# Last group's v with whole products P2 and P3, two copies moved to ScalarE, and no opening products of zeros: a two-layer graph network

## The chip, the cores and the metric

The kernel runs on one core of a Trainium2 chip, in one launch, in float32 throughout. The metric is the device time of one execution in microseconds (us). TensorE (PE) multiplies, VectorE (DVE), ScalarE (ACT) and GpSimd (POOL) work on tiles, and SyncE (SP) issues the DMAs. Each engine takes its own instructions strictly in the written order and waits where one of them needs the result of another engine.

## The reference

The inputs are `x` (128 graphs, 128 nodes, 512 features) and one symmetric 128x128 matrix `adj` of zeros and ones. Two layers follow one another, each with a residual and a normalization over the features:

```python
# layer 0
q = einsum('bnd,ed->bne', x, Wq); k = ...Wk; v = ...Wv
rel = adjacency.T * einsum('bnd,bmd->bnm', q, k)
rel = rel / norm(rel, axis=2)
x = layernorm(x + einsum('bnm,bmd->bnd', rel, v))
# layer 1: 8 heads of 64
q, k, v = x @ Wq + bq, x @ Wk + bk, x @ Wv + bv
w = softmax(q k^T / 8 + mask(adj), per head)
x = layernorm(x + w v)
```

## The kernel before, in words

**Groups and rounds.** The 128 graphs are cut into 32 groups of four, so that a group has 512 tokens and every projection is a 512x512x512 product. In a round of the schedule, layer 0 of the next group and layer 1 of the present one are interleaved. Layer 0 needs two projections: `m` (x times the product of Wq and Wk, which the kernel builds once at the start as M, line 200) and `v0`. Layer 1 needs `q`, `k` and `v1`.

**A projection** is class `Projection`. It is done in Winograd's form with seven products P1 to P7 of 256x256x256 blocks in place of eight, in the order 1, 5, 6, 2, 3, 7, 4 (`step`, lines 437 to 474). One such product is four matmuls of 128x128 weights against 256 columns (`product`, line 365). It needs sums of weight blocks (`weight_sums`, lines 156 to 160) and of token blocks (`token_sums`, lines 225 to 232), and VectorE or ScalarE folds its PSUM bank into the output. Products P2 and P3 need no sums and are split once more: each becomes seven products of 128x128x128 (`inner`, line 408; matmul in line 406), whose results VectorE adds in small pieces (lines 412 and 432), six additions for P2 and six for P3. This needs sums of 128x128 weight blocks (`inner_weight_sums`, line 148), and the last of these writes over the block `w[3]` of the weights themselves (line 154). Where `self.plain` is set, P2 and P3 are whole products with one addition each (lines 455 to 466); that is so for `m` and `v0` of group 0 alone.

**Order.** Everything is issued under a manual schedule. `dense` gives each projection step a position, and `short` gives every other piece of work one (`at`, line 778); a round is 35 positions long, and the pieces are issued by rising position, so the position decides the order on every engine's queue at once. The tables `ZERO`, `STEADY`, `QUICK` (round of the group before the last) and `LAST` (last group) hold the positions. PSUM tiles come from two pools that rotate, `ps_a` with two buffers and `ps_m` with six.

**The start.** `layer0_weights` (lines 178 to 204) first fills a tile with zeros and multiplies it by itself four times on TensorE into a bank that nobody reads. Then VectorE and ScalarE reorder the four chunks of Wq as they arrive, VectorE transposes the four quarters of Wv (line 192), transposes the first quarter of the first group's x (`x_transpose(0, 0, 0)`, line 194, instruction at line 219), and computes the sums of the Wv blocks (lines 157 to 160). TensorE meanwhile builds M. The other three quarters of x follow from the schedule.

**The end.** The last group has no later work to lie beside. Its softmax weights are transposed on TensorE against the identity (line 691) rather than by way of DRAM: two transposed halves `pwT` per graph, each copied from PSUM to SBUF (line 693). Seven of these eight copies are VectorE's, and the last one is ScalarE's. Per graph `b` the work is: scores (line 669), masking (674) and maximum (677) on VectorE, exponentials on ScalarE (684), transposition, products with v (708), scaling by the sums (713), residual (715 or 717), statistics (504, 505), the small steps of the standard deviation on GpSimd (509 to 519), normalization and store. In the same stretch the four graphs of the group before are finished (lines 607 to 654).

Of the kernel before, what the change touches and what calls it, by code (L numbers as in the profile page):

```python
# [8 lines left out]
F32 = mybir.dt.float32  # L9
# [9 lines left out]
def kernel(  # L19
# [122 lines left out]
    def inner_weight(key, o, i):  # L142
        if i >= 5:
            return wd[key][:, o - 2, i - 5]
        e, d = {1: (0, 0), 2: (0, 1), 3: (1, 0), 4: (1, 1)}[i]
        return wc[key][:, o - 1, d, e * P:(e + 1) * P]

    def inner_weight_sums(key, eng):
        for o in (2, 3):
            w = [None] + [inner_weight(key, o, i) for i in range(1, 8)]  # L150
            eng.tensor_tensor(w[5], w[3], w[4], op=ALU.add)
            eng.tensor_tensor(w[6], w[5], w[1], op=ALU.subtract)
            eng.tensor_tensor(w[7], w[1], w[3], op=ALU.subtract)
            eng.tensor_tensor(w[3], w[2], w[6], op=ALU.subtract)
# [21 lines left out]
    v21 = two.tile([P, 2, HF], F32, tag="wT", name="v21")  # L176

    def layer0_weights():

        z = one.tile([P, HF], F32, tag="wl", name="zeros")  # L180
        nc.gpsimd.memset(z, 0.0)
        pz = ps_m.tile([P, HF], F32, tag="m", name="pz")
        for _ in range(4):
            nc.tensor.matmul(pz, z[:, :P], z, start=True, stop=True)
        wq_p = one.tile([P, C, C, A, Q], F32, tag="v1", name="wq0_p")
        for ec in range(C):
            copy = nc.scalar.copy if ec % 2 else nc.vector.tensor_copy
            copy(wq_p[:, ec], quadrants(wq_s[:, ec]))
        for h in range(2):
            for dh in range(2):  # L190
                dst = wc["v0"][:, 3 if h else 1] if dh else v21 if h else wc["v0"][:, 0]
                nc.vector.transpose(dst.rearrange("p c (t s) -> p c t s", s=Q),
                                    wv_s[:, h, :, :, 2 * dh:2 * dh + 2, :].rearrange("p b a c r -> p c (b a) r"))
        x_transpose(0, 0, 0)
        weight_sums(wc["v0"], v21, nc.vector)
        p = [ps_a.tile([P, D], F32, tag="a", name=f"pM_{dc}") if dc < 2 else
             ps_m.tile([P, D], F32, tag="m", name=f"pM_{dc}") for dc in range(C)]
        for ec in range(C):
            for dc in range(C):
                nc.tensor.matmul(p[dc], wq_p[:, ec, dc].rearrange("p q r -> p (q r)"), quadrants(wk_s[:, ec]),  # L200
                                 start=(ec == 0), stop=(ec == C - 1))
        for dc in range(C):
            for e in range(2):
                place(wc["m"], m21, dc, e, p[dc][:, e * HF:(e + 1) * HF], nc.scalar.copy)
# [43 lines left out]
    def x_transpose(g, dh, h):  # L248
        if dh == 0 and h == 0:

            XT[g] = one.tile([P, C, G, P], F32, tag="xT" if g else "x1T", name=f"xT_{g}")
        if dh == 0 and h == 1:
            TX[g] = one.tile([P, 4, 2, HF], F32, tag="tx" if g else "tx1", name=f"tx_{g}")
        if dh == 1 and h == 0 and g:
            UX[g] = one.tile([P, 2, 4, P], F32, tag="ux", name=f"ux_{g}")
        transpose_quarter(XT[g], g, h, dh)
        if dh == 1 and g:
            inner_token_sums(UX[g], XT[g], 2 + h)
        if h:
            token_sums(TX[g], XT[g], dh, nc.gpsimd if g > 1 else nc.vector)  # L260
# [55 lines left out]
    class Projection:  # L316
# [8 lines left out]
        def begin(self):  # L325
            k, g = self.kind, self.g
            x0 = k in ("m", "v0")
            self.xT, self.t = (XT[g], TX[g]) if x0 else (X1T[g], TX1[g])

            self.plain = x0 and g == 0  # L330

            self.late = k == "v1" and g < NG - 1
            if self.late:
                self.s0 = one.tile([P, 2, HF], F32, tag="rel", name=f"s0_{self.name}")
            else:
                self.place()
                self.s0 = self.out(0, 0)
# [348 lines left out]
    def last_transpose(g, b, s):  # L686
        if b % 2 == 0 and s == 0:
            LT[b // 2] = one.tile([P, 2, H, P], F32, tag="tx1" if b else "x1T", name=f"wT_{g}_{b}")
        p = ps_m.tile([P, H // 2, P], F32, tag="m", name=f"pwT_{g}_{b}_{s}")
        for a in range(H // 2):  # L690
            nc.tensor.transpose(p[:, a, :], SOFT[g, b][0][:, s * (H // 2) + a, :], ident)
        copy = nc.scalar.copy if b == G - 1 and s else nc.vector.tensor_copy
        copy(LT[b // 2][:, b % 2, s * (H // 2):(s + 1) * (H // 2), :], p)

    def last_out(g, b, s):
# [37 lines left out]
    def last_store(g, b):  # L733
# [20 lines left out]
        (49, (50.5, 55, 55, 55, 55), (56.5, 58), 60.5, (64.5, 67, 69, 74.5, 76, 82, 83, 85.5)),  # L754
    )
    QUICK = (
        (31.5, (32, 33.5, 34.5, 34.5, 35), (35, 38), 40.5, (41, 43.5, 43.5, 47.5, 48.5, 50.5, 50.5, 52.5)),
        (36, (37, 37, 37, 37, 37), (39.5, 40.5), 41.5, (44.5, 45.5, 47.5, 50, 52, 53, 55, 62)),
        (37, (37.5, 41, 41, 41, 41), (41, 41), 45.5, (47.5, 50, 57.5, 57.5, 57.5, 59, 59.5, 64)),
        (37, (39, 41.5, 42.5, 44, 47), (44, 47), 49.5, (51, 52, 57.5, 61, 61, 64.5, 68.5, 68.5)),  # L760
    )
    LAST = (
        (17, (17, 17.5), (22, 22), (24, 24.5), 29, 35, 37.5),
        (17.5, (18, 19.5), (24, 25), (28.5, 33.5), 40.5, 48.5, 48.5),
        (19.5, (20, 23.5), (28.5, 29), (31, 37), 41.5, 51, 51.5),
        (23, (26.5, 26.5), (30.5, 31), (33.5, 41.5), 51, 51, 52.5),
    )


# [8 lines left out]
    def at(r, k, f, *a):  # L778
        short.setdefault(R * r + k, []).append((f, a))
# [14 lines left out]
    for g in range(NG):  # L794

        for h in range(2):
            if g:
                at(g - 2, 12, load_staged, g, h)
                at(g - 1, 12 + 4 * h, load, g, h)
        last = g == NG - 1  # L800

        sc, no, ou, de, ln, sp, st, tr = ZERO[0 if g == 0 else 2 if last else 1]
        for h in range(2):
            at(g - 1, sp[h], x1_spill, g, h)
            at(g - 1, st[h], x1_stage, g, h)
        for i, (dh, h) in enumerate(halves):
            if g or i:
                at(g - 2, ((25.5, 27, 28.5, 30) if g != 1 else (22, 23, 24, 25))[i], x_transpose, g, dh, h)
            at(g - 1, tr[i], x1_transpose, g, dh, h)
        for b in range(G):  # L810
            at(g - 1, sc[b], l0_score, g, b)
            at(g - 1, ou[b], l0_out, g, b)
            at(g - 1, ln[b // 2], l0_layernorm, g, b)
        at(g - 1, no, l0_norm, g)
        at(g - 1, de, l0_rstd, g)

        if last:
            at(g, 2, last_residual, g)
        for b in range(G):
            if last:  # L820
                sc, e, t, o, st, no, w = LAST[b]
                at(g, sc, last_scores, g, b)
                for i in range(2):
                    at(g, e[i], last_exp, g, b, i)
                    at(g, t[i], last_transpose, g, b, i)
                    at(g, o[i], last_out, g, b, i)
                at(g, st, last_stats, g, b)
                at(g, no, last_norm, g, b)
                at(g, w, last_store, g, b)
                continue  # L830
            s, ex, sp, st, pk = QUICK[b] if g == NG - 2 else STEADY[b]
            at(g, s, attn_scores, g, b)
            at(g, ex[0], attn_max, g, b)
            for i in range(4):
                at(g, ex[i + 1], attn_exp, g, b, 2 * i)
            for i in range(2):
                at(g, sp[i], attn_spill, g, b, i)
            at(g, st, attn_stage, g, b)
            pieces = attn_transpose, attn_out, attn_back, attn_rows, attn_sum, attn_stats, attn_norm, attn_write
            for k, f in zip(pk, pieces):  # L840
                at(g, k, f, g, b)
                if f is attn_rows:
                    at(g, RES if g < NG - 2 and b < 2 else k, attn_res, g, b)
# [3 lines left out]
    for k, name, eng in ((9, "v0", nc.vector), (17, "m", nc.vector), (28, "q", nc.gpsimd), (49.5, "k", nc.gpsimd),  # L847
                         (52, "v1", nc.gpsimd)):
        at(-1, k, inner_weight_sums, name, eng)

    with tc.manual_schedule():
        layer0_weights()
        for k in sorted({*short, *dense}):
            if k == -R:
                weight_sums(wc["m"], m21, nc.vector)
                for name, key in (("v", "v1"), ("q", "q")):
                    layer1_weights(name, key)
            for f, a in short.get(k, ()):
                f(*a)
            if k in dense:  # L860
                pr, i = dense[k]
                pr.step(i)
# [29 lines left out]
```

## Time and profile before

| | |
|---|---|
| median of five executions | 2450.43 us (2445.81 to 2452.06) |
| the profiled execution, time | 2451.07 us |
| its span, first to last instruction | 2449.1 us |
| TensorE busy in the span | 2425.7 us (99%) |
| VectorE busy | 1975.6 us (81%) |
| ScalarE busy | 1012.6 us (41%) |
| GpSimd busy | 1139.9 us (47%) |
| mean granted TensorE clock | 0.996 |

A float32 matmul appears in the trace as two passes, each a weight load (PEld) and a MATMUL, so the four matmuls of one product are eight records ("x8"). Records on TensorE overlap, since one starts before the one ahead has drained; how fast TensorE goes is read from the distance of the starts, not from the mean duration. A line of the timeline gives the start, the duration, the engine, the line of the kernel and the operation with its operands, and in brackets how long the engine had been idle and what it waited for. The chain view follows the work that ended last back through its releasers. The stretch view gives the busy time of each engine in a stretch, then the granted clock, the share of the DMA engines and the bytes.

### The profile page before, as it was taken

To read this page: it belongs to the slowest core of one execution; us is meant where nothing else is said; L and a number is where in the kernel's file an instruction comes from. 1 tells how busy PE (TensorE), PEld (TensorE's weight loads), DVE (VectorE), ACT (ScalarE), POOL (GpSimd) and SP (SyncE) were. 2 spreads that over 40 slices of the span, in tenths; PEclk is the share of its full clock that TensorE was granted. 3 is DMA by queue.
4 is the path that set the end of the run, shared out by engine and by line. 5 is a ranking of instruction groups with operands and counts; after the bars stand their busy time and mean duration, and the time that the engine had idled before them with its cause. 6 is when DMAs were issued, how large, how long until landed. Compare 5 with 4: busy or idle time off the path is not lost.

```text
span 2449.1 us, 48459 instructions
## 1 busy us (share of the span) xinstructions
PE 2425.7 (99%) x16560; PEld 2136.1 (87%) x16560; DVE 1975.6 (81%) x4409; ACT 1012.6 (41%) x3211; POOL 1139.9 (47%) x1797
## 2 busy tenths in 40 slices
PE   8999999999999999999999999999999999999997
PEld 6889888888888898888888888888888888888886
DVE  6678888788888788887888887888878888878887
ACT  1234443443444443444434434434444344344354
POOL 3625535345444455343454344553444543435544
PEclk9999999999999999999999999999999999999999
DMA  7356665666565666556665656665656656566564
GB/s 160 93 132 168 175 176 160 177 168 164 171 180 156 171 173 176 170 164 172 173 166 169 180 156 169 173 173 168 173 164 173 166 173 179 157 171 174 153 174 128
DMA packets 508600, 405.17 MB, mean 165 GB/s; under 512 B 37568, under 2 KB 424768, under 8 KB 508352
## 3 DMA queue, kind: packets, MB, share of 16 engines
q1 hardware_dynamic: 508352, 402.08, 59.7%
q8 instruction: 129, 2.11, 0.4%
q14 instruction: 119, 0.97, 0.1%
HBM read 237.31 MB, written 164.63 MB: 164 GB/s over the span
## 4 chain that ended last, share of the span: by engine, by line
PE 96%; DVE 2%; issue 0%; DMA 0%; SPq 0%; POOL 0%; POOLq 0%; ACT 0%; DVEq 0%
PE pa_v L365 18%; PE pa_q L365 9%; PE pa_m L365 9%; PE pa_k L365 9%; PE pc_v L406 8%; PE ps L549 5%; PE po L607 5%; PE pst L484 5%; PE pb_v L365 5%; PE po L529 4%; PE pc_k L406 4%; PE pc_q L406 4%; PE pc_m L406 4%; PE pb_q L365 2%; PE pb_k L365 2%; PE pb_m L365 2%
## 5 line engine op out<-in xcount | busy, mean ns | idle before, releaser
L575 ACT ACTIVATE w<-w,nmax 128x128 f32<-128x128 f32 x992 | 384.0, 395 | 116.0 <-DVE nmax L568 115.9
L509 POOL TENSOR_SCALAR ve<-st 128x1 f32<-128x1 f32 (+1 forms) x160 | 46.0, 287 | 746.2 <-DVE st L505 735.1
L365 PE MATMUL pa_v<-wc_v,tx 128*128 128x256 f32 x1536 | 363.8, 380 | 0.0
L365 PEld LDWEIGHTS pa_v<-wc_v,tx 128*128 128x128 f32 x1536 | 277.2, 190 | 30.9 <-issue 0.6
L524 ACT ACTIVATE xr<-xr,sh,rstd 128x512 f32<-128x512 f32 x58 | 47.2, 815 | 411.4 <-POOL sh L519 411.4
L575 ACT ACTIVATION_READ_ACCUMULATOR w<-w,nmax 128x1 f32 x992 | 191.8, 193 | 0.0
L365 PE MATMUL pa_m<-tx,wc_m 128*128 128x256 f32 x768 | 186.8, 387 | 3.2 <-DVE yT L461 2.2
L412 DVE TENSOR_TENSOR v<-pc_v,v 128x256 f32<-128x256 f32 (+1 forms) x444 | 135.2, 310 | 58.3 <-PE pc_v L406 46.4
L365 PEld LDWEIGHTS pa_q<-tx,wc_q 128*128 128x128 f32 x768 | 143.2, 190 | 44.4 <-issue 29.3
L365 PE MATMUL pa_k<-tx,wc_k 128*128 128x256 f32 x768 | 181.8, 380 | 0.0
L365 PE MATMUL pa_q<-tx,wc_q 128*128 128x256 f32 x768 | 181.6, 379 | 0.2 <-DVE qT L461 0.2
L558 DVE SCALAR_TENSOR_TENSOR w<-ps,mask 128x512 f32<-128x512 f32 x248 | 153.2, 680 | 7.3 <-PE ps L549 7.3
L365 PEld LDWEIGHTS pa_m<-tx,wc_m 128*128 128x128 f32 x768 | 140.1, 192 | 20.1 <-DVE yT L461 2.6
L568 DVE TENSOR_REDUCE nmax<-w 128x4 f32<-128x512 f32 x248 | 157.2, 675 | 0.0
L594 DVE STREAM_TRANSPOSE wT<-wl 128x1024 f32<-128x1024 f32 x124 | 154.0, 1242 | 0.3 <-DMA xl_x<-in_x_dram 0.3
L365 PEld LDWEIGHTS pa_k<-tx,wc_k 128*128 128x128 f32 x768 | 138.4, 190 | 14.9
L638 POOL TENSOR_TENSOR xr<-xr,bv_b 128x512 f32<-128x512 f32 x58 | 73.8, 1272 | 144.8 <-DMA xr<-x1d 83.9
L376 ACT ACTIVATE qT<-pa_q,bq_sb 128x256 f32<-128x256 f32 x128 | 53.7, 471 | 204.9 <-PE pa_q L365 200.2
L406 PE MATMUL pc_v<-wd_v,ux 128*128 128x128 f32 x756 | 135.8, 275 | 0.2 <-DVE v L412 0.2
L412 DVE TENSOR_TENSOR qT<-pc_q,qT 128x128 f32<-128x128 f32 (+1 forms) x320 | 96.5, 309 | 44.4 <-PE pc_q L406 36.7
L529 PE MATMUL po<-v,rel 128*128 128x512 f32 x256 | 130.7, 594 | 0.0
L549 PE MATMUL ps<-kT,qT 64*128 64x128 f32 x1984 | 129.5, 279 | 0.0
(231 smaller groups left out, 6180.9 us busy)
## 6 DMA issues: line engine op xcount, KB each, us to landing
wd<-w SPq DMA_DIRECT2D x248, 256.0 KB, 3.1
wl<-wd SPq DMA_DIRECT2D x496, 128.0 KB, 3.1
xl_x<-in_x_dram SPq DMA_DIRECT2D x256, 128.0 KB, 5.9
x<-in_x_dram SPq DMA_DIRECT2D x64, 512.0 KB, 4.7
x1d<-x SPq DMA_DIRECT2D x64, 512.0 KB, 3.1
xl_h<-x1d SPq DMA_DIRECT2D x256, 128.0 KB, 2.9
od<-oT SPq DMA_DIRECT2D x496, 64.0 KB, 2.1
o<-od SPq DMA_DIRECT2D x118, 256.0 KB, 3.0
```

The source lines that it names most:

```text
L365: nc.tensor.matmul(bank[:, m, :], l[:, k, m * P:(m + 1) * P], r[:, k, :], start=start and m == 0 and k == 0, stop=(m == 1 and k == 1), ski ...
L406: nc.tensor.matmul(self.c[o][:, slot, :], l, r, start=start, stop=True, skip_group_check=True)
L412: nc.vector.tensor_tensor(y, self.c[o][:, slot], s if kept else y, op=ALU.add)
L484: nc.tensor.matmul(p, XT[g][:, dc, b, :], YT[g][:, dc, b, :], start=(dc == 0), stop=(dc == C - 1))
L529: nc.tensor.matmul(p, REL[g][0][:, b, :], V0[g][:, b, :], start=True, stop=True)
L549: nc.tensor.matmul(p[s][:, :, a, :], QT[g][r, a, b, :], KT[g][r, a, b, :], start=True, stop=True)
L558: nc.vector.scalar_tensor_tensor(w[:, s].rearrange("p q a r -> p (q a r)"), p[s].rearrange("p q a r -> p (q a r)"), HD ** -0.5, mask, op0= ...
L568: nc.vector.tensor_reduce(nmax[:, s * (H // 2):(s + 1) * (H // 2)], w[:, s].rearrange("p q a r -> p a q r"), axis=AX.XY, op=ALU.max, negat ...
L575: nc.scalar.activation(w[:, s, :, a, :], w[:, s, :, a, :], AF.Exp, bias=nmax[:, i:i + 1], accum_out=sums[:, i:i + 1])
L594: nc.vector.transpose(wT, SOFT[g, b][0].rearrange("p a i r -> p i a r"))
L607: nc.tensor.matmul(p[s * HD:(s + 1) * HD, a, :], V1[g][:, b, h * HD:(h + 1) * HD], wT[:, s * (H // 2) + a].rearrange("p q t -> p (q t)"), ...
L638: nc.gpsimd.tensor_tensor(xr, xr, bv_b, op=ALU.add)
```

## The change

Five things change. The opening zeros and their four products go. The first quarter of x of group 0 is no longer transposed ahead of the sums of the Wv blocks; it is issued from the schedule with the other three, behind them. `v1` of the last group is `plain`: P2 and P3 are whole products. As the weight block `w[3]` has been written over by then, two 128x128 blocks of it are copied aside on GpSimd when the sums are made, and copied back on GpSimd in the last round. Of the eight copies of transposed softmax weights in the last group ScalarE takes three instead of one: the second half of graph 2 and both of graph 3. Last, the positions in `QUICK` and `LAST` are set anew.

```diff
+    kept = const.tile([P, 2, P], F32, name="kept")
+    def restore(key):
+        for o in (2, 3):
+            nc.gpsimd.tensor_copy(inner_weight(key, o, 3), kept[:, o - 2])
     def inner_weight_sums(key, eng):
         for o in (2, 3):
             w = [None] + [inner_weight(key, o, i) for i in range(1, 8)]
+            if key == "v1":
+                eng.tensor_copy(kept[:, o - 2], w[3])
...
     def layer0_weights():
-        z = one.tile([P, HF], F32, tag="wl", name="zeros")
-        nc.gpsimd.memset(z, 0.0)
-        pz = ps_m.tile([P, HF], F32, tag="m", name="pz")
-        for _ in range(4):
-            nc.tensor.matmul(pz, z[:, :P], z, start=True, stop=True)
...
-        x_transpose(0, 0, 0)
         weight_sums(wc["v0"], v21, nc.vector)
...
-            self.plain = x0 and g == 0
+            self.plain = (x0 and g == 0) or (k == "v1" and g == NG - 1)
...
-        copy = nc.scalar.copy if b == G - 1 and s else nc.vector.tensor_copy
+        copy = nc.scalar.copy if b + s >= G - 1 else nc.vector.tensor_copy
...
     QUICK = (
-        (31.5, (32, 33.5, 34.5, 34.5, 35), (35, 38), 40.5, (41, 43.5, 43.5, 47.5, 48.5, 50.5, 50.5, 52.5)),
-        (36, (37, 37, 37, 37, 37), (39.5, 40.5), 41.5, (44.5, 45.5, 47.5, 50, 52, 53, 55, 62)),
-        (37, (37.5, 41, 41, 41, 41), (41, 41), 45.5, (47.5, 50, 57.5, 57.5, 57.5, 59, 59.5, 64)),
-        (37, (39, 41.5, 42.5, 44, 47), (44, 47), 49.5, (51, 52, 57.5, 61, 61, 64.5, 68.5, 68.5)),
+        (31.5, (32, 33.5, 34.5, 34.5, 34.5), (35, 37.5), 40.5, (40.5, 43.5, 43.5, 47.5, 48.5, 50.5, 51.5, 52.5)),
+        (36, (37, 37, 37, 37, 37), (39.5, 40.5), 41.5, (44.5, 45.5, 47.5, 50, 52, 53, 55, 61.5)),
+        (37, (37.5, 41, 41, 41.5, 41.5), (41, 41.5), 45.5, (47.5, 49.5, 57.5, 57.5, 57.5, 59, 59, 66)),
+        (37, (39, 41.5, 42.5, 46, 47), (44, 47), 49.5, (51, 52.5, 57.5, 61, 61, 65.5, 68.5, 68.5)),
     )
     LAST = (
-        (17, (17, 17.5), (22, 22), (24, 24.5), 29, 35, 37.5),
-        (17.5, (18, 19.5), (24, 25), (28.5, 33.5), 40.5, 48.5, 48.5),
-        (19.5, (20, 23.5), (28.5, 29), (31, 37), 41.5, 51, 51.5),
-        (23, (26.5, 26.5), (30.5, 31), (33.5, 41.5), 51, 51, 52.5),
+        (17, (17, 17.5), (22, 22.5), (24.5, 29), 33.5, 39, 39),
+        (17.5, (18, 19), (24.5, 24.5), (28, 33.5), 40, 49, 49),
+        (19.5, (19.5, 23.5), (29, 29), (31, 37), 41.5, 51, 51.5),
+        (23, (26.5, 26.5), (30.5, 33), (34, 45.5), 51.5, 51.5, 53),
     )
...
-            if g or i:
-                at(g - 2, ((25.5, 27, 28.5, 30) if g != 1 else (22, 23, 24, 25))[i], x_transpose, g, dh, h)
+            at(g - 2, ((25.5, 27, 28.5, 30) if g != 1 else (22, 23, 24, 25))[i], x_transpose, g, dh, h)
...
+    at(NG - 1, 4, restore, "v1")
```

On the queues this comes out as follows. TensorE's order is the same up to the last 60 or so instructions, but for the four products of zeros. In the last round the 14 small matmuls of v go; P2 and P3 stand together between the scores of graph 1 and those of graph 2; the last attention product of the group before (line 607) stands behind P6 instead of ahead of the first scores. VectorE loses twelve additions (lines 412 and 432) and two copies (line 693) there and gains two additions (lines 458 and 466). On ScalarE the bias copy of k's last quarter (line 376) stands ahead of a normalization (line 524) instead of behind it.

## The prediction

> **What bounds the kernel now.** I read the page first. TensorE is busy for 99% of the span, and the chain of waits is TensorE for 96%:
>
> ```profile
> PE 2425.7 (99%) x16560; PEld 2136.1 (87%) x16560; DVE 1975.6 (81%) x4409; ACT 1012.6 (41%) x3211; POOL 1139.9 (47%) x1797
> PE 96%; DVE 2%; issue 0%; DMA 0%; SPq 0%; POOL 0%; POOLq 0%; ACT 0%; DVEq 0%
> ```
>
> In the stretches 100 to 170, 170 to 240, 240 to 310 and 2300 to 2370 us TensorE is busy for all 70 us. The change touches nothing there, so only the start and the last 45 us can move the time. I took the timeline of both next. At the start:
>
> ```profile
> 1.23 3.59 PE L184 MATMUL pz<-zeros 128*128 128x256 f32 x8 [1.23 <-POOL zeros L181]
> 4.66 13.90 PE L200 MATMUL pM<-wk_s,wq_p 128*128 128x512 f32 x32
> 18.35 0.71 DVE L219 STREAM_TRANSPOSE xT<-xl_x 128x512 f32<-128x512 f32 x1
> 19.21 1.97 PE L365 MATMUL pa_v<-wc_v,xT 128*128 128x256 f32 x8 [0.65 <-DVE xT L219]
> 22.22 0.69 DVE L228 TENSOR_TENSOR tx<-xT 128x512 f32<-128x512 f32 x1
> 22.97 1.99 PE L365 MATMUL pb_v<-wc_v,tx 128*128 128x256 f32 x8 [1.80 <-DVE tx L228]
> ```
>
> The eight passes of zeros start 0.43 us apart, although later passes of this size take 0.22 (a product of eight is 1.73 long from start to start). So TensorE runs at half rate until 4.66 and at full rate from the first pass of M (512 columns in 0.43). The clock column says 1.00 from 0 us on; here the durations decide. After M, TensorE waits for VectorE twice.
>
> At the end the chain leaves TensorE for VectorE at 2407.9 and comes back to it only for short pieces:
>
> ```profile
> 2407.17 0.68 PE pc_v L406 x6
> ...
> 2407.94 0.44 DVE v L412
> ...
> 2421.13 0.21 DVE v L432
> 2421.34 0.04 issue
> 2421.38 1.22 PE pc_v L406 x4
> 2422.60 2.06 PE ps L669 x16
> 2424.66 1.28 DVE w L674 x2
> ...
> 2445.39 0.55 DVE o L731
> ```
>
> What TensorE waits for there, and the clock (the figure behind the five busy times), in the timeline and by stretches:
>
> ```profile
> 2421.38 1.22 PE L406 MATMUL pc_v<-wc_v,ux 128*128 128x128 f32 x4 [1.89 <-DVE v L432]
> 2418.00:2420.00 2.00, 1.36 (x10) 1.12 (x10) 1.97 (x4) 2.00 (x12) 1.85 (x4) 1.00 0.58 139
> 2420.00:2422.00 2.00, 0.62 (x3) 0.62 (x4) 2.00 (x5) 2.00 (x8) 0.33 (x1) 0.78 0.54 208
> 2422.00:2424.00 2.00, 2.00 (x17) 1.77 (x18) 1.72 (x5) 0.26 (x2) 0.55 (x1) 0.50 0.12 46
> ```
>
> VectorE is full, TensorE stands idle for 1.89 us behind an addition (line 432), and right after that its clock is halved for some 3.4 us: the scores of graph 3 take 2.0 us from start to start of the next, where those of graph 0 took 1.09.
>
> **The change, part by part.**
>
> *Zeros removed.* The half rate now falls on M. Cold stretches in this trace: 3.4 us (1.23 to 4.66), 3.4 us (2421.2 to 2424.6) and 6.8 us (45.5 to 52.3, where the clock reads 0.50). At half rate M loses half of that, 1.7 to 3.4 us, and ends at 20.3 to 22.0 instead of 18.6. M can't start sooner to any use, as the next step shows.
>
> The Trainium skill says why this speaks against the change ("TensorE: Matmul & The Clock Gate", "Part 1"): the array begins at half clock and is let up after a busy window of about 3.4 us that runs free of the kernel, so the cold time falls between one and two windows. By that rule alone M would be 1.7 to 3.4 us late and the sum would be worse by as much; by the rows most of it is covered.
>
> *First transposition moved.* VectorE is busy without a gap from 15.72 to 31 us, so the moved instruction changes its order there and not its load. The four sums (18.99 to 21.48, 2.49 us) now come first, and the transposition ends at 18.3 + 2.5 + 0.7 = 21.5 instead of 19.06. P1 of v0 (pa_v) starts 0.15 behind it, as before: 21.65 instead of 19.21. That covers the late M up to 2.95 us; beyond it (M ending at 22.0) up to 0.5 us shows. The token difference (line 228) still ends at 22.85, but P5 (pb_v) must wait for P1: 21.65 + 1.83 = 23.5 instead of 22.97. P6 follows at 25.3 instead of 25.00, since there it was a VectorE result at 24.85 that set it. From P6 on TensorE is unbroken to 42 us, and the VectorE addition at 32.25 waits for it. So the start costs 0.3 us, and 0.3 to 0.8 with the cold bound. Nothing later has slack to take it back: TensorE's 70 us stretches are full.
>
> *Copies aside and back on GpSimd.* A 128x128 copy on GpSimd is not in the trace; 128x512 copies take 0.61, additions of 128x128 take 0.46. I take 0.45 each (0.15 to 0.6). The first two lie at 101 to 105 us, with 5.86 us of GpSimd idle behind them; the last two go into the idle 1.81 us ahead of line 509 at 2386.2, and P2 needs them 26 us later. Queued behind each pair are the small steps of line 509, whose inputs come later than the pair ends. Cost nothing; were the cover gone, 0.9 us.
>
> *QUICK.* Up to 2407 us this exchanges neighbours: on VectorE a transposition (line 594) with a scaling (636), on ScalarE a bias copy with exponentials, on SP one spill with a staging. TensorE lost 0.19 us in the 37 us from 2370, so there is little to win; lost could be a late operand. I take 0, between -0.2 and +0.5.
>
> *The last group.* On TensorE 14 small matmuls at 0.22 (3.1 us) become two products of 1.73 (3.5 us): 0.4 more, against 1.89 and 0.17 of idle time and the cold stretch that go. On VectorE twelve additions go, by start-to-start distances 1.34 + 0.52 + 0.50 + 0.39 + 0.48 = 3.2 us; two of 0.60 come; two copies of 0.60 go to ScalarE. Net 3.2 us less on the engine that carries the chain. As the order changes too, I laid the new order out with the distances of the old rows (masking 0.62, maximum 1.15, additions and copies 0.60, statistics 0.8, scaling with reciprocal 0.55; on TensorE 1.83 for a product that can't load ahead, 1.05 for scores). The points on the way:
>
> | start of | before | after |
> |---|---|---|
> | masking, graph 0 | 2410.65 | 2408.5 |
> | masking, graph 1 | 2414.23 | 2412.6 |
> | masking, graph 2 | 2418.00 | 2417.3 |
> | masking, graph 3 | 2424.64 | 2422.1 |
> | copy of v's last quarter (ACT) | 2426.57 | 2423.1 |
> | exponentials, graph 3 | 2430.29 | 2427.7 |
> | last statistics | 2443.13 | 2438.2 |
>
> Graph 0: scores at 2407.0 right behind P4 of k; their third and fourth pairs wait for ScalarE's copy of k, which now ends at 2408.0, so masking starts at 2408.5 rather than behind the additions. Graph 2: P2 and P3 stand ahead of its scores (2412.4 + 1.83 + 1.73 + 1.1), so TensorE gives most of the lead back; this is what is late next. Graph 3: VectorE passes from the maximum of graph 2 (2418.5) through one addition, two copies and a scaling to 2422.1, and the scores run at full clock. Then ScalarE: exponentials of graph 3 end at 2430.9, three copies at 0.60 end at 2432.7, products and scaling follow, and the last statistics come 4.9 us early. ScalarE's added 1.2 us lie in that chain already. Taken: 4.9. The low end is 2.0 (the 3.2 us of VectorE's work less 1.2 if ScalarE's copies delay the last graph in full); the high end 6.2 (two of the GpSimd collisions of before, line 636 at 1.27 instead of 0.68 and line 715 at 1.16 instead of 0.42, go as well).
>
> Sum: +0.3 - 4.9 = -4.6 us against the profiled 2451.07, which is 0.64 above the median: **2445.8** for the median of 2450.43. About 0.2% (4.9 us) is what a measurement of this kernel can tell from no change, so the forecast lies just inside it.
>
> **Rivals.**
>
> 1. *The tail keeps only part.* P2 and P3 hold up the scores of graph 2 and then ScalarE the last graph; TensorE idles between the late products and goes cold again (the idle before 2421 halved it), and pieces of 0.5 us double. For: TensorE's rows after 2427 are short and broken by waits. Against: the clock stayed at 1.00 from 2424.6 to 2441 with just such gaps. Gain 2.5, net -2.2: 2448.2.
> 2. *More than laid out.* Both collisions go: net -5.9: 2444.5. For: line 715 alone takes 0.42. Against: the additions of line 717 stand as close to it in the new order.
> 3. *Slower: M stays cold.* If the clock is not let up while M runs, its 32 passes take 0.85 each and it ends at 32 instead of 18.6; P1 starts 10.3 us later than 21.65, and the result is 2451.07 - 0.64 - 4.6 + 10.3 = 2456. It decides from 16 us of cold on (half of it, less the 2.95 covered, must outweigh 4.9). Against: the longest cold stretch here is 6.8 us.
> 4. *The steady part shifts.* The bank of the zeros is no longer taken, so the rotation of `ps_m` is one on, and `kept` moves the tiles. Against: the same buffers are waited for in the same order. 0.1% either way: 2443.4 or 2448.3.
>
> **How the numbers follow.** Likeliest case 0.55, rival 1 0.22, rival 2 0.14, rival 3 0.03, rival 4 0.06. Faster by over 0.2% means under 2445.5: rival 2, not quite half of the likeliest case, part of rival 4: 0.42. Slower by over 0.2%: rival 3 and a late operand under QUICK, 0.05. Within: 0.53. The range runs from 2443.6 (rival 2 and some of the scatter) to 2449.0 (rival 1 with the start at +0.8).
>
> **What would show it.** Passes of M 0.85 us apart at first, P1 of v0 at about 21.7 behind line 219, P6 0.3 later than 25.0. No 1.89 us idle on TensorE near 2421, full clock through the scores of graph 3, masking of graph 3 some 2.5 us earlier against the start of the round, and the last statistics 4 to 5 us earlier. It is wrong if P2 waits for the copies back, if M runs cold beyond 6 us, or if the masking of graph 2 comes later than before.

## The result and the profile after

| | before | after |
|---|---|---|
| median, all executions | 2448.86 us (44; 2445.14 to 2452.7) | 2445.81 us (26; 2442.1 to 2449.4) |
| ratio of times | | 0.9989, 95% interval 0.9983 to 0.9994 |
| the profiled execution, time | 2451.07 us | 2444.39 us |
| its span | 2449.1 us | 2442.6 us |
| mean granted TensorE clock in it | 0.996 | 0.998 |

The change makes the kernel about 2.7 us faster (1.5 to 4.2 by the interval; 3.05 by the two medians): a real gain, but inside the 0.2% that was named as the bound of "no change". The two profiled executions differ by more, 6.5 us of span, and most of this chapter is about why.

The page of the changed kernel, busy times and the chain of waits by engine, reads almost as before. TensorE still sets the time, with 20 records and 6.9 us of busy time less:

```profile
PE 2418.8 (99%) x16540; PEld 2133.4 (87%) x16540; DVE 1972.5 (81%) x4397; ACT 1013.2 (41%) x3213; POOL 1139.7 (47%) x1800
PE 97%; DVE 2%; DMA 1%; issue 0%; POOL 0%; SPq 0%; POOLq 0%; ACT 0%; DVEq 0%
```

**Two anchors divide the span.** P5 of `k` (`pb_k`) is in every round. Its start in group 0 and its start in the last group lie 2281.98 to 2282.04 us apart in before, in after and in the four kernels of the first experiments. So the steady part is unchanged within 0.06 us, and the 6.5 us are 3.5 at the start (P5 of `k` in group 0 at 102.14 instead of 105.70, less that 0.06) and 3.0 in the end (from the last P5 of `k` to the end of the span: 58.43 instead of 61.42).

**The start.** The timeline of after, its first products on TensorE, and VectorE's first transposition of Wv (start, duration, engine, line, operands, count, idle time and its cause in brackets):

```profile
4.41 15.66 PE L202 MATMUL pM<-wk_s,wq_p 128*128 128x512 f32 x32 [4.41 <-DMA wk_s<-in_L_gnn_Wk_dram]
23.14 1.97 PE L367 MATMUL pa_v<-wc_v,xT 128*128 128x256 f32 x8 [3.07 <-DVE xT L221]
24.94 1.89 PE L367 MATMUL pb_v<-wc_v,tx 128*128 128x256 f32 x8
26.66 0.60 PE L367 MATMUL pa_v<-wc_v,tx 128*128 128x256 f32 x2
```
```profile
17.22 1.30 DVE L195 STREAM_TRANSPOSE wc_v<-wv_s 128x512 f32<-128x512 f32 x2 [8.78 <-DMA wv_s<-in_L_gnn_Wv_dram]
```

M takes 15.66 us instead of 13.90, and its first pass at full rate starts at 7.89. The pass ahead of that one took 0.78 us from start to start, where the full ones at half rate took 0.86, so the rate came up at about 7.81 (an estimate). So some 3.40 us at half rate fall on M and cost it 1.76 us, and it ends at 20.07. Nothing waits for that: P1 of `v0` stands 3.07 us longer, until VectorE has made `xT`. P1 comes at 23.14 because Wv itself arrived later in this execution (transposition at 17.22 instead of 15.72); from that transposition to P1 it is 5.92 us.

Next, the stretch behind the first group's first products, by stretches (busy time and count of PE, PEld, DVE, ACT, POOL, then the granted clock, the DMA share and GB/s). First before, then after:

```profile
46.00:52.00 6.00, 5.15 (x13) 3.61 (x12) 2.66 (x9) 0.00 (x0) 0.00 (x0) 0.50 0.01 1
58.00:64.00 6.00, 5.18 (x12) 3.56 (x13) 4.78 (x8) 0.59 (x1) 4.09 (x8) 0.72 0.00 0
```
```profile
46.00:52.00 6.00, 4.91 (x28) 4.02 (x27) 3.50 (x11) 0.58 (x1) 1.10 (x1) 1.00 0.05 11
58.00:64.00 6.00, 6.00 (x23) 3.81 (x22) 5.83 (x10) 1.66 (x3) 5.18 (x10) 1.00 0.01 3
```

Read the figure behind the five busy times and the count of TensorE's records together. Before spent 6.83 us from 45.5 and 3.41 us from 59.1 at half clock and got 13 and 12 passes through; after was at full clock, with 28 and 23. From P6 of `v0` to P5 of `k` it is 80.70 us in before and 75.48 in after, 5.22 less; half of the 10.24 us at half clock would be 5.1. Less the 1.50 us that Wv was late in after, and the 0.16 by which P6 stands later behind Wv's first transposition (9.44 us instead of 9.28), this gives 3.56, which is the whole lead at P5 of `k`. The change touches nothing there: whether TensorE is at half clock at 45 and 59 us has to be explained by itself.

**The end.** After, TensorE and then VectorE in the last round. The rows answer those of 2407 to 2445 us of before:

```profile
2417.68 1.99 PE L367 MATMUL pa_v<-wc_v,tx 128*128 128x256 f32 x8
...
2420.85 1.04 PE L693 MATMUL pwT<-ident,w 128*128 128x128 f32 x8
2423.34 2.70 PE L710 MATMUL po<-v,wT 128*128 128x64 f32 x16 [1.45 <-DVE wT L695]
2425.84 2.46 PE L693 MATMUL pwT<-ident,w 128*128 128x128 f32 x12
2428.14 1.00 PE L710 MATMUL po<-v,wT 128*128 128x64 f32 x8
```
```profile
2418.75 1.28 DVE L676 SCALAR_TENSOR_TENSOR w<-ps,maskp 128x512 f32<-128x512 f32 x2
...
2423.80 1.60 DVE L638 TENSOR_TENSOR wc_m<-wc_m,rs 128x512 f32<-128x512 f32 x1
...
2429.18 0.42 DVE L715 TENSOR_TENSOR o<-po,rs 128x256 f32<-128x256 f32 x1 [0.68 <-PE po L710]
...
2436.61 0.69 DVE L506 BATCH_NORM_STATS2 bs<-o 128x6 f32<-128x512 f32 x1
```
```profile
2420.00:2424.00 4.00, 2.27 (x19) 1.96 (x18) 3.83 (x9) 2.18 (x10) 1.58 (x5) 1.00 0.11 41
2424.00:2428.00 4.00, 4.00 (x24) 4.00 (x23) 3.50 (x7) 3.78 (x18) 3.32 (x3) 0.57 0.18 68
```

The 1.89 us of idle time ahead of the scores of graph 3 are gone, and these scores run at full clock (1.09 us from their start at 2416.59 to the next). But TensorE is idle for 1.45 us a little later, behind VectorE's copy (line 695), is busy for 2.27 of the 4 us from 2420, and then has 0.57 of its clock from 2424 to 2428: the cold stretch has moved, by 6.8 us against the last P5 of `k` (from 33.5 us behind it to 40.3), and not gone. The scaling in line 638 takes 1.60 beside an addition of GpSimd (the first row), where it took 1.27 in before (line 636 there, the second row) and 0.68 elsewhere:

```profile
2423.58 1.28 POOL L640 TENSOR_TENSOR wc_v<-wc_v,bv_b 128x512 f32<-128x512 f32 x1
```
```profile
2430.84 1.27 DVE L636 TENSOR_TENSOR wc_m<-wc_m,rs 128x512 f32<-128x512 f32 x1
```

### The profile page after: what moved, and what is told of

Read it like the earlier page. It is cut to its first block, busy times and chain, and to the rows that moved or that the text cites. A ratio compares the mean times of both kernels' runs of the same rounds, so it can differ in the third digit from the quotient of the medians.

```text
span 2442.6 us, 48413 instructions
## 1 busy us (share of the span) xinstructions
PE 2418.8 (99%) x16540; PEld 2133.4 (87%) x16540; DVE 1972.5 (81%) x4397; ACT 1013.2 (41%) x3213; POOL 1139.7 (47%) x1800
## 4 chain that ended last, share of the span: by engine, by line
PE 97%; DVE 2%; DMA 1%; issue 0%; POOL 0%; SPq 0%; POOLq 0%; ACT 0%; DVEq 0%
PE pa_v L367 18%; PE pa_q L367 9%; PE pa_k L367 9%; PE pa_m L367 9%; PE pc_v L408 8%; PE ps L551 5%; PE po L609 5%; PE pst L486 5%; PE pb_v L367 5%; PE po L531 4%; PE pc_k L408 4%; PE pc_q L408 4%; PE pc_m L408 4%; PE pb_q L367 2%; PE pb_k L367 2%; PE pb_m L367 2%
## 5 line engine op out<-in xcount | busy, mean ns | idle before, releaser
L414 DVE TENSOR_TENSOR v<-pc_v,v 128x256 f32<-128x256 f32 (+1 forms) x434 | 132.2, 310 | 57.2 <-PE pc_v L408 45.5
```

The lines of the kernel that those rows point to most:

```text
L414: nc.vector.tensor_tensor(y, self.c[o][:, slot], s if kept else y, op=ALU.add)
```

## The experiments

The predicted mechanism (**as laid out**) says: the start costs some tenths of a microsecond, plain P2 and P3 carry the end, the copies on ScalarE help, all in the order of the written plan. The rival (**clock**) says: what the profiles and times differ by is mostly where TensorE's half-clock stretches fall, and these follow its idle time, so that a part of the change seems worth more or less than it is. The first four runs split the change, the next four put the disputed costs aside, the last four split the change again with those costs gone. Times are medians; each ratio is against the kernel before, run beside it on the same chip. The three sets ran on three chips, so medians are compared within a set where that is possible. "The end" is the time from the last P5 of `k` to the end of the span, in one profiled execution each.

### Start alone, end alone

The new start (no zeros, transposition from the schedule) in the kernel before:

```diff
     def layer0_weights():
-        z = one.tile([P, HF], F32, tag="wl", name="zeros")
-        nc.gpsimd.memset(z, 0.0)
-        pz = ps_m.tile([P, HF], F32, tag="m", name="pz")
-        for _ in range(4):
-            nc.tensor.matmul(pz, z[:, :P], z, start=True, stop=True)
...
-        x_transpose(0, 0, 0)
...
-            if g or i:
-                at(g - 2, ..., x_transpose, g, dh, h)
+            at(g - 2, ..., x_transpose, g, dh, h)
```

> The kernel before with the change's start alone: no zeros, the first quarter of x behind the sums of Wv. In the profiled executions the changed kernel led by 3.5 us at P5 of k of the last group (2387.68 against 2384.18) and the first round had no half clock there. Theory 1 (the start costs 0.3 us as forecast; the 3.5 us are where the clock's halvings happened to fall in these two executions): +0.3 us on the median, 2449 against 2448.9, within plus or minus 1. Theory 2 (the new start itself keeps the clock up in the first round): about -3 us, and no stretch at half clock between 40 and 65 us of its profile.

Measured: 2450.59 us against 2447.93; ratio 1.0008 (0.9999 to 1.0018), that is +2.0 us (-0.2 to +4.4). M takes 16.39 us here and ends at 20.69; P1 of `v0` still waits 1.38 us for VectorE. From the first transposition of Wv to P6 of `v0` it is 9.44 us; in before it was 9.28. So the new start costs 0.16 us by the trace. The rest of the +2.0 is not seen as a cost of the start. The mean granted clock of the 12 executions was 0.9964, that of before beside them 0.9971, which accounts for a part of it, and the interval reaches down to nothing. By stretches of this kernel:

```profile
46.00:52.00 6.00, 5.15 (x14) 3.69 (x14) 3.32 (x11) 0.00 (x0) 0.00 (x0) 0.56 0.00 1
58.00:64.00 6.00, 4.89 (x19) 3.05 (x12) 4.62 (x8) 0.58 (x1) 3.63 (x7) 0.72 0.00 0
```

These are the same two stretches at half clock as in before (6.83 us from 46.7, 3.41 from 60.4), which the same start in after does not have. The removed zeros therefore neither cause nor cure them.

The other way round, the kernel after with the old start (the edit above undone in it):

> The changed kernel with the start of before: zeros and the early quarter of x are back. Theory 1: the whole gain is in the end, 3.0 us by the distance from P4 of k (2405.28 and 2401.77) to the end of the span (43.8 and 40.8 us), so 2445.5 or a little less than the changed kernel's 2445.8. Theory 2: the gain of the end is small and most of it goes away: 2448.

Measured: 2446.71; ratio 0.9996 (0.9987 to 1.0005), -1.0 us. In the profiled execution the end is 60.05 us long, 1.36 less than before and 1.62 more than in after, though the end's instructions are the same as in after: here 6.83 us from 2421.9 are at half clock instead of 3.41. Neither half of the change can be told from nothing at this spread, and their sum (+1.0, uncertain by some 3 us either way) neither agrees nor disagrees with what the whole gives (-2.7). Parts can't be added up from these times. What speaks for the clock is the end: the same instructions, and 1.62 us more with twice the time at half clock.

### The parts of the end

P2 and P3 of `v1` in small pieces again, in the new order and with the new copies:

```diff
-            self.plain = (x0 and g == 0) or (k == "v1" and g == NG - 1)
+            self.plain = x0 and g == 0
...
-    at(NG - 1, 4, restore, "v1")
```

> The changed kernel with v of the last group back on the small products (14 matmuls of 128 columns, twelve additions), positions and copies as changed. If P2 and P3 as whole products carry the gain of the end: two thirds of it go, +1.5 to +2.5 us against the changed kernel (2447.5 to 2448.3), with an idle stretch of TensorE behind an addition of v near the transpositions of graph 0. If the copies on ScalarE or the positions carry it: within 0.5 us of the changed kernel.

Measured: 2446.88; ratio 0.9995 (0.9985 to 1.0005). The end is 59.12 long and has no stretch at half clock before 2439 us this time. Plain products seem to carry 1.1 us by the medians against after, which was not timed beside it, so this is far from certain.

Two of the copies back on VectorE:

```diff
-        copy = nc.scalar.copy if b + s >= G - 1 else nc.vector.tensor_copy
+        copy = nc.scalar.copy if b == G - 1 and s else nc.vector.tensor_copy
```

> The changed kernel with the two copies of transposed softmax weights back on VectorE. If VectorE sets the end there: +0.6 to +1.2 us against the changed kernel (two copies of 0.60). If the scaling beside GpSimd and the halved clock around the products of graph 1 set it: 0 to +0.4 us.

Measured: 2446.12; ratio 0.9989 (0.998 to 0.9998), the same as the whole change. The end is 59.39 long, with one stretch of 3.41 at half clock as in after (58.43). By the times the copies seem worth nothing, by the end's length 0.96 us.

### Take the half clock and the collision away

If idle time on TensorE brings the half clock, then products that nobody reads, put into that idle time, must take it away without touching the kernel's work. Seven of them in the first group, where TensorE waits for VectorE:

```diff
+    def fill(n, pool, tag):
+        p = pool.tile([P, HF], F32, tag=tag, name="fill")
+        for _ in range(n):
+            nc.tensor.matmul(p, ident, bv_b[:, :HF], start=True, stop=True)
+    for k, n in ((12.9, 3), (15.9, 1), (21.9, 1), (34.9, 2)):
+        at(-1, k, fill, n, ps_m, "m")
```

> The changed kernel with seven matmuls whose result nobody reads (identity times the bias, 128x256, two passes each) put into TensorE's idle time of the first round: three ahead of P7 of m, one ahead of P4, one ahead of the column sums, two ahead of P1 of the next m. So far, at an equal granted clock, all kernels with the changed end have spans within 0.2 us of each other (2443.7 at 0.997), and each 0.001 of clock less goes with 1.6 to 2.3 us more. Theory 1 (the spread of some 8 us is where the clock gate's free windows of 3.4 us fall on TensorE's idle time near 45 and 59 us): no half clock there in its profile, highest time below 2447.5, median 2443 to 2444.5. Theory 2 (the clock drops for another reason, idle time is a symptom): spread 2442 to 2449 as without the filling, median 2445.8.

Measured: 2444.37 (2442.52 to 2447.31); ratio 0.9981 (0.9973 to 0.999). The timeline on TensorE, and the stretch:

```profile
43.35 1.53 PE L858 MATMUL fill<-bv_b,ident 128*128 128x256 f32 x6
45.98 2.00 PE L367 MATMUL pa_m<-tx,wc_m 128*128 128x256 f32 x8 [1.10 <-DVE yT L463]
47.81 0.59 PE L858 MATMUL fill<-bv_b,ident 128*128 128x256 f32 x2
```
```profile
46.00:52.00 6.00, 5.35 (x26) 4.35 (x27) 3.79 (x11) 0.58 (x1) 0.00 (x0) 1.00 0.07 14
```

No half clock is left between the start and 2424 us. One profile alone would not show much, since after, the end-only kernel and the next two below have none there either. But of all eight profiles without these fillers four have half clock near 46 us, and of the six with them none has. The end, which this edit doesn't touch, was unlucky in the profiled execution: 60.05, with 6.83 us at half clock from 2424.1.

The same in the end, three such products into the 1.45 us ahead of line 710:

```diff
+    at(NG - 1, 27.9, fill, 3, ps_a, "a")
```

> The changed kernel with three such matmuls ahead of the first products of graph 1 in the last group, where TensorE stood idle for 1.45 us and the clock was then halved from 2424.4 to 2427.9. Theory 1 (this half clock is a good part of the 1.9 us by which the end missed its forecast of 4.9): the distance from P5 of k of the last group to the end of the span falls from 58.4 to 57.0 to 57.8, and the median falls by 0.3 to 1.0 to about 2445. Theory 2 (VectorE's scaling beside GpSimd sets it): distance 58.1 to 58.5, no change.

Measured: 2445.03; ratio 0.9987 (0.9978 to 0.9995). The end is 57.68, 0.75 less than in after, and its clock stays full until 2433.5. TensorE's rows:

```profile
2420.73 1.46 PE L858 MATMUL fill<-bv_b,ident 128*128 128x256 f32 x6
2422.35 2.00 PE L710 MATMUL po<-v,wT 128*128 128x64 f32 x16 [0.16 <-DVE wT L695]
2424.18 1.48 PE L693 MATMUL pwT<-ident,w 128*128 128x128 f32 x12
```

Products with v and transpositions take 3.3 us where they took 4.8 (2423.34 to 2428.14) in after. Half of this is lost again: the scaling in line 638 still takes 1.59, and TensorE then waits 0.62 us for VectorE's next copy (line 695).

Next the collision: graph 3 of the group before gets its bias added on GpSimd a few microseconds earlier, so that no GpSimd addition lies beside that scaling.

```diff
+    def early_bias(g, b):
+        nc.gpsimd.tensor_tensor(EARLY[g, b], EARLY[g, b], bv_b, op=ALU.add)
...
-        nc.gpsimd.tensor_tensor(xr, xr, bv_b, op=ALU.add)
+        if (g, b) not in EARLY:
+            nc.gpsimd.tensor_tensor(xr, xr, bv_b, op=ALU.add)
...
+    at(NG - 2, 57.6, early_res, NG - 2, 3)
+    at(NG - 2, 58, early_bias, NG - 2, 3)
```

(`early_res` issues the load of that tile, as `attn_res` did.)

> The changed kernel with GpSimd's bias addition for the last graph of the group before moved ahead, into GpSimd's idle time before the small steps of graph 2 (its load is issued earlier too). In the changed kernel's profile VectorE's scaling at 2423.80 took 1.60 us beside this addition instead of 0.68. Theory 1 (the half clock): scaling back at 0.7, end nearly unchanged, 58.2 to 58.5 from P5 of k to the end. Theory 2 (the collision): scaling 0.7, and the distance falls by 0.6 to 1.0 to 57.4 to 57.8, the median to about 2445.

Measured: 2445.99; ratio 0.999 (0.9982 to 0.9999): nothing against after, and the end is 58.44. The scaling is short (the first row below), but VectorE then waits for TensorE, which is at half clock from 2423.4 (the second row):

```profile
2422.83 0.68 DVE L650 TENSOR_TENSOR wc_m<-wc_m,rs 128x512 f32<-128x512 f32 x1
...
2425.21 0.42 DVE L728 TENSOR_TENSOR o<-po,rs 128x256 f32<-128x256 f32 x1 [0.99 <-PE po L723]
```

The Trainium skill ("SBUF — State Buffer", "Who interferes with whom") says that a VectorE instruction with two inputs in SBUF contends with a GpSimd instruction that reads SBUF, over a pair of ports that one of them locks for itself. The rows agree: 1.60 and 1.59 beside the addition, 0.68 without it.

All three together:

> All three together, as the version that may beat both. If the two causes at the end add up: 56.3 to 57.0 us from P5 of k to the end, and with the first round at full clock a median of 2441.5 to 2443.5 and a highest time below 2446.5. If the chain has a third limit there (the last residuals and standard deviations on GpSimd): distance above 57.3.

Measured: 2442.61 (2441.05 to 2443.49); ratio 0.9974 (0.9965 to 0.9983). This is 5.6 us under the kernel before by the medians and the best of the versions so far; against the first group filled alone, on the same chip, it is 1.8 (2444.37 less 2442.61). The end is 57.10: by its length the half clock alone is worth 0.75, the collision alone nothing, both 1.33. Each hides in part behind the other: TensorE's late products and VectorE's late scaling meet in the products of graphs 1 and 2. What limits the end next was not tested. A candidate is GpSimd, whose two residual additions follow each other, and the statistics of VectorE wait for both, as they did in after (0.55 and 0.31 there too):

```profile
2429.98 2.69 POOL L732 TENSOR_TENSOR o<-o,x 128x512 f32<-128x512 f32 x2
```
```profile
2431.48 0.69 DVE L506 BATCH_NORM_STATS2 bs<-o 128x6 f32<-128x512 f32 x1 [0.55 <-POOL o L732]
2432.70 0.69 DVE L506 BATCH_NORM_STATS2 bs<-o 128x6 f32<-128x512 f32 x1 [0.31 <-POOL o L732]
```

### The parts again, with the clock quiet

With the fillers and the early bias in, one part each is undone in that best version: the plain products, the copies, the start. The edits are those shown above. The kernel before with the seven fillers of the first group stands beside them.

> The version with all three additions (2442.6 us, 57.1 us from P5 of k to the end, times within 2.4 us of each other), but v of the last group on the small products again. At an equal granted clock of 0.997 the earlier run of this step gave 2444.9 against 2443.7. Theory: whole products P2 and P3 carry 1.2 to 2.0 us of the end's gain, the rest being the new positions: median 2443.8 to 2444.6, distance 58.3 to 59.1. Rival: they carry all of it: 2445.3 or more.

> The same version with the two copies of transposed softmax weights back on VectorE. Theory (VectorE sets the end now that the half clock and the collision are out of the way): +0.6 to +1.2 us, median 2443.2 to 2443.8. Rival (the end waits for ScalarE's exponentials of graph 3 and the products behind them, not for VectorE): within 0.4 us of 2442.6, or below it.

> The same version with the start of before: zeros, and the first quarter of x ahead of the sums. The forecast says that the new start costs 0.3 us (P6 of v0 stood 9.44 us behind the transposition of the first Wv quarter in four profiles of the new start, 9.28 and 9.06 in two of the old): median 2442.1 to 2442.5. Rival (the half clock on M costs more than was covered): 2441.7 or less.

> The kernel before with the seven fillers of the first round alone. If the clock's halving there is a property of TensorE's idle time and not of the change: highest time below 2450, no half clock between 40 and 65 us, median about 1.5 to 2.5 us below before, 2445.8 to 2446.7. If the fillers only help the changed start: no change, 2448.

| version | median, us | ratio (95%) | end, us |
|---|---|---|---|
| without plain products | 2444.93 | 0.9984 (0.9975 to 0.9993) | 58.53 |
| copies back on VectorE | 2443.92 | 0.9977 (0.9968 to 0.9985) | 57.93 |
| old start | 2442.54 | 0.9973 (0.9962 to 0.9983) | 56.93 |
| before, first group filled | 2446.82 | 0.9989 (0.998 to 0.9998) | 61.37 |

The three variants are read against the old-start version, since all of the table ran on one chip, and the whole best version ran on another (its ratio there is 0.9974, that of the old start here 0.9973). By the traces the old start is 0.27 us shorter (9.17 us from Wv's transposition to P6, 9.44 in the other two), and the differences of the medians below contain that; those of the end's length do not. So:

- Plain products are worth 2.4 us (2444.93 less 2442.54; 1.6 by the end's length), and the fastest execution without them (2443.05) was slower than the slowest of the old-start version (2442.97). Without them the wait that they were to remove is back, on the first row of TensorE's small products:

```profile
2418.23 0.71 PE L408 MATMUL pc_v<-wc_v,ux 128*128 128x128 f32 x4 [1.88 <-DVE v L434]
```

- The copies on ScalarE are worth 1.4 us (1.0 by the end's length), not nothing. In after itself the end's length gave nearly as much (0.96), half clock and collision included: what hid the gain there was the scatter of the times.
- The start costs nothing that the times can tell: new 0.9974, old 0.9973, each with some 0.001 (2 us) either way.
- The fillers alone bring the kernel before 2.8 us (2449.63 to 2446.82; 0.5 to 4.9 by the interval), without a change to its work.

Without plain products the end is still 58.53 where the kernel before had 61.37. That 2.8 us belongs to the other edits together: the copies (1.0 of it, if they are worth as much there), the positions in `LAST`, the early bias and the filler in the end. What the positions carry alone was not measured.

## Why the prediction was right, and where not

**The time** was forecast at 2445.8 and is 2445.81; the likeliest outcome, a gain inside 0.2%, is what came. But the sum was not as good as this looks. It was subtracted from a median over five executions, 2450.43; over 44 it is 2448.86. The forecast gain was 4.6 us, the measured one is 2.7 (1.5 to 4.2; 3.05 by the medians). The base was 1.6 us too high and the gain as much too large, and that the two errors cancelled is luck. As a gain, 4.6 lies outside the interval, and the 2.2 of rival 1 lies inside it. The remark that the profiled execution lay 0.64 above the median fell with it: it lay 2.2 above, and that of after 1.4 below its own median, which is 3.6 of the 6.7 us between the two profiled times.

**Zeros removed.** Right. M was to lose 1.7 to 3.4 us and lost 1.76 in after, and 1.61 to 2.99 in the ten profiles with the new start. It was to be covered by VectorE up to 2.95, and P1 of `v0` waited for VectorE in all ten, by 0.24 us (where M took longest, 16.89) to 3.07.

**First transposition moved.** Right. It was to cost 0.3 us; from the first transposition of Wv to P6 of `v0` it cost 0.16 (9.28 to 9.44), or 0.38 against the end-only kernel's 9.06. From Wv's transposition to P1 it was to be 5.93 us and was 5.92. The times show no cost.

**Copies aside and back, QUICK.** Costed at nothing. Each copy took 0.29 us (0.45 was the estimate), the last two at 2380.8, some 28 us ahead of P2. The copies back go with plain products, whose undoing took them out too, so their cost is inside the 2.4 us net; the copies aside were never undone. The middle distance did not move, so nothing of `QUICK` that lies before the last P5 of `k` cost anything; by itself it was not measured.

**The last group.** The order was laid out well and the last step mis-sized. The start of each landmark, counted from the last P5 of `k` and put on the scale of before (3.50 added to after's times):

| start of | forecast | measured |
|---|---|---|
| masking, graph 0 | 2408.5 | 2408.61 |
| masking, graph 1 | 2412.6 | 2412.65 |
| masking, graph 2 | 2417.3 | 2417.40 |
| masking, graph 3 | 2422.1 | 2422.25 |
| copy of v's last quarter | 2423.1 | 2423.22 |
| exponentials, graph 3 | 2427.7 | 2427.89 |
| last statistics | 2438.2 | 2440.11 |

Six points are within 0.2 us, the last one is 1.9 late. So the term of -4.9 measured -3.0 (1.36 in the end-only run and in the one with the first group filled, where the half clock lasted twice as long). The step that failed is the one from the exponentials to the last statistics, "come 4.9 us early": durations at full clock and an uncollided scaling were used there. What stands in its place was shown by taking it away: TensorE cold from 2424.4 and the scaling at 1.60, together 1.3 us of the 1.9 by the end's length. The remaining 0.6 was not isolated; the chain there runs over GpSimd's two additions.

**Rivals.** Rival 1's mechanism came true in part: TensorE idled, went cold again, and its products and transpositions took 4.8 us where they took 3.3 at full clock. What was put against it, that the clock stayed at 1.00 through just such gaps in before, was true of those gaps and not a reason: 1.45 us of idle time were enough here. Rival 2 came by half: the collision on line 638 stayed (1.60 after 1.27), the one on line 715 of before went (0.42 after 1.16, line 717 of after). Rival 3 did not come; M was cold for 3.40 us in after and, by its length, for about 6 at most. Rival 4 fell with the constant middle distance.

## What to carry to other kernels

Compare two profiles between anchors that the change can't touch before reading a gain off their spans; here 3.5 of 6.5 us lay where the change had no part, in TensorE's clock and in Wv's arrival. When an idle gap on TensorE goes, look for the next thin stretch as well: here the half clock went there, and the small products behind it took half as long again. Two costs on two engines can hide each other (0.75 us and nothing alone, 1.33 together here), so take both away before calling either free.

## What the runs showed that was not expected

**The scatter of this kernel is its clock.** Executions of before ran from 2444.7 to 2453.5 us in the first two sets, and their mean spans fall in the order of the granted clock: 2443.7 us at a clock of 0.999 (17 executions), 2446.5 at 0.997 (14), 2449.9 at 0.995 (8), 2451.3 at 0.994 (2). The fillers close the spread: 7.3 us in after (2442.1 to 2449.4, 26 executions), 4.8 with the first group filled (12), 2.4 with all of the edits (10). In before, filling the first group took it from 5.5 us (2446.31 to 2451.78, 29 executions) to 2.1 (11).

**A gap well short of the window is enough.** Apart from the last, which runs on to the end of the kernel, the half-clock stretches are 3.41 or 6.83 us long in all traces, one window or two. Before each, the window was thin, not empty: TensorE was busy for about 36% of 42.1 to 45.5, 42% of 55.7 to 59.1 and 47% of 2417.7 to 2421.1 in before, with single gaps of 0.86 to 2.17 us, and the clock was halved each time. The window from 2431.4 to 2434.8, about 70% busy, stayed at full clock, and one about 75% busy from 45.5, already at half clock, was not let up. But the busy share alone doesn't decide. In after the window ahead of the half clock, 2421.0 to 2424.4, was about 58% busy; with all three edits one about 79% busy from 2428.5, which held transpositions and small products, was followed by half clock; and with the early bias one only 44% busy, from 40.9 (counted back in whole windows from the later half clock), was not. What the clock goes by stays open. The Trainium skill ("TensorE: Matmul & The Clock Gate", "HAM oscillation — how this bites in real kernels") gives the rule that gaps over about 3.4 us bring the clock down. The runs agree on the length of the window and not on the gap: gaps of 1 to 2 us were enough here. Its remark that the window runs free of the kernel (same page, "Part 1") fits what the scatter shows, the same work with the half clock in one execution and not in the next. It fits the times of the changes too: in before they come at 45.46, 59.12, 2421.14 and 2441.62, whole multiples of 3.413 us apart (4, 692 and 6). The end of the half rate at the start, about 4.51 in before (the last pass of zeros took 0.28 us instead of 0.43) and 7.81 in after (both estimates), lies 708 such windows ahead of 2421.14 and of 2424.44, the first halvings of the end.

**The clock column is silent at the start.** It reads 1.00 from 0 us in every trace, although the first passes go at half rate (the zeros 0.43 us apart in before, M slow until about 7.81 in after). There the distance of the starts has to be read.
